# Folding softmax sums to 16 rows per unit by two chains of transfers

## The chip, the cores and the metric

The kernel runs on one core of a Trainium2 chip. Its metric is the device time of one execution in microseconds. The kernel before takes 2106.54 us (median of 3 runs, 2106.08 to 2106.72).

The core has five engines that run beside each other, each through its own list of instructions in order: TensorE (PE, matmuls), VectorE (DVE), ScalarE (ACT), GpSimd (POOL) and SyncE (SP), which here only issues transfers. [...] Memory on the chip has 128 partitions (rows).

## The reference

Two layers on 8 images of 512 channels and 32x32 positions (N = 1024), all in float32. The first is attention with 8 heads, the second a non-local block with a batch norm at its end.

```python
q = _conv1x1(x, Wq, bq).reshape(B, h, d, H * W)
k = _conv1x1(x, Wk, bk).reshape(B, h, d, H * W)
v = _conv1x1(x, Wv, bv).reshape(B, h, d, H * W)
attn = jax.nn.softmax(jnp.einsum('bhdn,bhdm->bhnm', q, k) * scale, axis=-1)
out = jnp.einsum('bhnm,bhdm->bhdn', attn, v).reshape(B, C, H, W)
return x + _conv1x1(out, Wp, bp)
...
f_div_C = jnp.einsum('bcn,bdn->bcd', theta_x, phi_x) / n
y = jnp.einsum('bcd,bdn->bcn', f_div_C, g_x).reshape(b, C_INTER, h, w)
z = _conv1x1(y, W_w, W_b) + x
mean = jnp.mean(z, axis=(0, 2, 3), keepdims=True)
var = jnp.var(z, axis=(0, 2, 3), keepdims=True)
z_hat = (z - mean) * jax.lax.rsqrt(var + EPS)
```

The change is in the softmax alone: in how the sums over the keys, by which the output of attention is divided, are added up.

## The kernel before

The images are taken one after the other. For each, the projections q, v and k are made by products that save multiplications in Strassen's manner (`six`, L377, for the images after the first; each loads its weights by SP in pieces as the ring `wr` comes free, L160 to L175 and L186). Then comes `attention` (L575), then the output projection and the second layer.

Attention goes through 8 units of two heads and 512 queries, and each unit through 8 blocks of 128 keys. For a block TensorE makes the scores with the keys in the rows (L601), ScalarE takes the exponential (L604) into a tile of 128 rows and 2 x 512 columns, and VectorE adds it to the unit's `acc` (L608, L610). TensorE multiplies the exponentials with v (L627). No maximum is taken off; a check of the sums decides at the end whether a second, shifted version has to run.

After a unit's last block, `acc` holds, in each of its 128 rows, sums over 8 keys. The sum over the 128 rows is still to be taken, and `spread` (L642) prepares it: `acc` is cut into four quarters of 32 rows; SP copies the first to 32 rows of the tile `fold` (L638) and POOL adds the other three to it by three transfers (L640), each of which waits until the one before has landed. Unit u goes to the rows from 32 (u mod 4) and to operand u div 4 of the tile, 1024 columns each. So units 0 to 3 fill the 128 rows of one operand, and 4 to 7 those of the next. The last image (`make_f` is set) takes another path for its last unit, and makes its denominators in two halves.

The denominators of an image are then a product with a matrix of zeros and ones (`folds4`, L512), which adds the 32 rows of each unit: `all_denominators` (L670) calls `in_tiles` (L662) with two operands, four matmuls each, one for each quarter of the 1024 columns. A matmul writes 32 rows of `den`. VectorE takes the reciprocals (L678), they go to device memory (L680) and come back spread over the rows (L721), and POOL multiplies the output of attention with them (L707).

This product doesn't stand at the end of attention. It is one of the `fills` of the next image's q (L1107): in `six`, ahead of the third pair of products, two additions are put on POOL (L423, L424) and then the denominators are made. TensorE, VectorE and these POOL additions keep the order of the program (`pe` and `dve`, L62 to L65). Transfers are placed by a scheduler, which leaves each engine a fixed list: on SP, behind the last copy of an image's sums, the first piece of the next k's weights (256 KB) and then two pieces of v's weights (896 KB each); on POOL, the accumulates of all units and then the additions of q.

The tile `fold` has one buffer, `acc` three. `folds4` is made once at the start by VectorE.

Of the kernel before, what the change touches and what calls it, by code (L numbers as in the profile page):

```python
# [8 lines left out]
F32 = mybir.dt.float32  # L9
I32 = mybir.dt.int32  # L10
AF = mybir.ActivationFunctionType
ALU = mybir.AluOpType
# [4 lines left out]
P = 128  # L17
HEADS = 8
# [4 lines left out]
def attention_nonlocal_kernel(tc: tile.TileContext, a: dict, out: bass.AP):  # L23

    sound = unshifted(tc, a, out)
    with tc.If(sound < P):
        shifted(tc, a, out)
# [3 lines left out]
def unshifted(ctx: ExitStack, tc: tile.TileContext, a: dict, out: bass.AP):  # L31
    nc = tc.nc
# [5 lines left out]
    D = C // HEADS  # L38
# [8 lines left out]
    const = ctx.enter_context(tc.tile_pool(name="const", bufs=1))  # L47
# [14 lines left out]
    def pe(ins):  # L62
        tc.keep_in_program_order(ins)

    dve = sp = pe  # L65
# [10 lines left out]
    def block(name):  # L76
        return ring.tile([P, 2, 512], F32, tag="e", name=name)
# [25 lines left out]
    def weight_sums(w, a21, which=(3, 4, 5, 6), pin=lambda ins: None, engine=None):  # L103
        for to, l, r, op in ((3, a21, w[2], ALU.add), (4, w[3], w[0], ALU.subtract),
                             (5, w[0], a21, ALU.subtract), (6, w[1], w[4], ALU.subtract)):
            if to in which:
                pin((engine or nc.vector).tensor_tensor(w[to], l, r, op))
# [83 lines left out]
    def weights(name, sums_done=False, pin=lambda ins: None):  # L191

        w = loaded.pop(0)
        assert w.name == name
        if name not in kept and name != "tp":
            if not sums_done:
                weight_sums(w, corner[name], pin=pin)
            keep("plain" if name == "WpT" else name, w)
        return w
# [42 lines left out]
    def bias_product(t, ps):  # L242
        for oc in range(CC):
            pe(nc.tensor.matmul(ps[:, oc:oc + 1], t[:, oc * P:(oc + 1) * P], ones, start=True, stop=True,
                                skip_group_check=True))
        got = small.tile([P, CC], F32, tag="got", name="got")
        nc.scalar.copy(got, ps)
        nc.vector.tensor_tensor(bp, bp, got, ALU.add)
# [234 lines left out]
    for x_part, w_part in (((0, 1, 0), (w_first[0], 0, 0, 0, 1)), ((1, 2, 0), (w_first[0], 0, 0, 1, 2)),  # L483
# [3 lines left out]
        at = slice(h * 512, (h + 1) * 512)  # L487
        nc.sync.dma_start(xt[:, c0:c1, at], x_v[0, :, c0:c1, at])
        if w_part:
            to, m, k, c0, c1 = w_part  # L490
# [18 lines left out]
    nc.vector.memset(folds8, 0.0)  # L509
    for i in range(4):  # L510
        nc.vector.memset(folds8[i * P // 4:(i + 1) * P // 4, i * 8:(i + 1) * 8], 1.0)
    folds4 = const.tile([P, D], F32, tag="folds4", name="folds4")  # L512
    nc.vector.memset(folds4, 0.0)
    for i in range(4):
        for at in (i * 4, P // 4 + 16 + i * 4):
            nc.vector.memset(folds4[i * P // 4:(i + 1) * P // 4, at:at + 4], 1.0)
    mv = const.tile([P, CC, 2], F32, tag="mv", name="mv")
    ngamma = const.tile([P, CC], F32, tag="ngamma", name="ngamma")
    spill = [dram.tile([P, CC, N], F32, tag=f"spill{b}", name=f"spill{b}") for b in range(B - LATE + 1)]
# [7 lines left out]
    def heads_of(b, what, w, bias, data, pin=lambda ins: None, steps=None, fills=None, **how):  # L527

        t = mats.tile([P, CC, N], F32, tag=what, name=f"{what}_{b}")

        if fills is not None:
            def begin(to, ps, i):
                nc.scalar.activation(to, ps, AF.Identity, bias=bias[:, i:i + 1])

            def third(to, ps, of, i):
                if what == "q":
                    nc.scalar.activation(to, ps, AF.Identity, bias=steps[:, i:i + 1])
                else:
                    dve(nc.vector.scalar_tensor_tensor(to, ps, steps[:, i:i + 1], of, ALU.add, ALU.add))

            six(f"p{what}_{b}", w, data, False, lambda q: t[:, rows(q), cols(q)], begin, third, fills,
                what == "q")
            return t

        def first(q, ps):
            for m in range(2):
                c = rows(q).start + m
                if how.get("early") and q == "21":
                    nc.vector.tensor_scalar(t[:, c, cols(q)], ps[:, m, :], bias[:, c:c + 1], 1.0, ALU.add, ALU.mult)
                else:  # L550
                    nc.scalar.activation(t[:, c, cols(q)], ps[:, m, :], AF.Identity, bias=bias[:, c:c + 1])

        seven(f"p{what}_{b}", w, data, False, first, add_to(t, pin), **how)

        return t
# [19 lines left out]
    def attention(b, q, k, v, near_end, make_f=None):  # L575
# [7 lines left out]
        units = [(p, h) for p in range(NPAIR) for h in range(NH)]  # L583
# [53 lines left out]
        def together(to, parts):  # L637
            nc.sync.dma_start(to, parts[0])  # L638
            for part_of in parts[1:]:
                nc.gpsimd.dma_start(to, part_of, accum_op=ALU.add)  # L640

        def spread(u, pin=lambda ins: None, meanwhile=lambda: None):  # L642

            g, i = divmod(u, 4)
            acc = accs.pop(u).rearrange("p j n -> p (j n)")
            if u == 0:
                folded["t"] = foldp.tile([P, 4, 1024], F32, tag="fold", name=f"fold_{b}")
            t = folded["t"]  # L650
            to = t[i * P // 4:(i + 1) * P // 4]
            parts = [acc[k * P // 4:(k + 1) * P // 4, :] for k in range(4)]
            if make_f and u == len(units) - 1:
                for k in range(4):
                    (nc.scalar if k % 2 else nc.sync).dma_start(to[:, (k + 1) % 4, :], parts[k])
                meanwhile()
                for l, r in ((1, 2), (3, 0), (1, 3)):
                    pin(nc.vector.tensor_tensor(to[:, l], to[:, l], to[:, r], ALU.add))
                return
            together(to[:, g, :], parts)  # L660

        def in_tiles(ps, sums):  # L662

            of = P // 4
            for n, (lhsT, t) in enumerate(sums):
                for i in range(4):
                    pe(nc.tensor.matmul(ps[i * of:(i + 1) * of, :], lhsT, t[:, i * 256:(i + 1) * 256],
                                        start=(n == 0), stop=(n == len(sums) - 1), skip_group_check=True))

        def all_denominators(ps):  # L670

            t = folded.pop("t")
            if b == 0:
                bias_product(t[:, 3, :], ps[:, 1, :CC])
            den = ps[:, 0, :256]
            in_tiles(den, [(folds4[:, g * P // 4:(g + 1) * P // 4], t[:, g, :]) for g in range(2)])
            ri = t[:, 2, :256]
            dve(nc.vector.reciprocal(ri, den))  # L678
            d = dram.tile([P // 4, 256], F32, tag=f"den{b}", name=f"den_d_{b}")
            nc.scalar.dma_start(d, ri.rearrange("(x s) n -> x s n", s=4)[:, 0, :])  # L680
            own.append((slice(b * 64, (b + 1) * 64), d.rearrange("x (y n) -> (x y) n", y=4)))
            return d.rearrange("(j k x) m -> j k (x m)", j=2, k=2)
# [66 lines left out]
        if make_f:  # L749
            return o["o"], lambda ps: denominators(1, ps), lambda d: normalize((first_den, d))  # L750
        return o["o"], all_denominators, normalize

    def project(b, xt, w, between, data):
# [271 lines left out]
    t = [block(f"t{i}_x_0") for i in range(4)]  # L1025
# [17 lines left out]
    k = heads_of(0, "k", wk, bk, data, dve)  # L1043
# [10 lines left out]
    for b in range(B):  # L1054
# [46 lines left out]
        if not last:  # L1101
# [15 lines left out]
            else:  # L1117
                w_p = loaded[1]
                more = [lambda i=i: weight_sums(w_p, corner["WpT"], (i,), dve, nc.gpsimd) for i in (3, 4, 5)]
            k = heads_of(b + 1, "k", weights("WkT"), bk, data, dve, steps=dk, fills={  # L1120
                (0, 13): [*o_sums, *(more if b else ())], (1, 13): () if b else more,
                (2, 0): () if b else [lambda: weight_sums(w_p, corner["WpT"], (6,), dve, nc.gpsimd)]})
# [305 lines left out]
```

## Time and profile before

| what | value |
|---|---|
| median of the runs | 2106.54 us |
| the profiled execution | 2106.07 us |
| its span | 2104.3 us |
| TensorE busy | 2082.4 us, 99% |
| VectorE busy | 1428.2 us, 68% |
| ScalarE busy | 789.9 us, 38% |
| POOL busy | 584.9 us, 28% |
| accumulating transfers of POOL (L640) | 189 of 128 KB, 767 ns of POOL each, 3.0 us to landing (median) |
| copies of SP (L638) | 63 of 128 KB, 2.3 us to landing (median) |
| matmuls of the denominators (L667) | 128 records in 8 images, 379 ns each |

The span reaches from the first to the last instruction of the program; the execution has 1.8 us around it. A float32 matmul[...] has two records. The duration of a matmul is longer than the distance to the next one, since they overlap. In the timeline a line has its start, its length, the engine, the line of the source, the operation and the tiles (out<-in); the brackets give the idle time of the engine before it and what ended that time. For transfers, the length is that of the issue on the engine, and the time from issue to landing is given apart.

### The profile page before, as it was taken

The page shows a single profiled execution, that of the slowest core. Times are in us where ns is not written, and L with a number is a line of the kernel's source. Part 1 is how long each engine was busy: PE and PEld are TensorE (multiplying, and loading weights), DVE is VectorE, ACT ScalarE, POOL GpSimd, SP SyncE. Part 2 cuts the span into 40 slices and gives each one's busy share as a digit, 9 for nine tenths or more (in the row PEclk, how much of TensorE's full clock was granted, in tenths as well). Part 3 has the DMA queues.
Part 4 walks back from the last instruction along what each step waited for, and adds up shares of the span by engine and source line. Part 5 has one row for each costly group of instructions (what it writes and reads, how often), then busy time and mean ns, then how long its engine had stood idle before and what let it go on. Part 6 is the DMA issues. An engine that isn't in the chain of part 4 may idle for free.

```text
span 2104.3 us, 33849 instructions
## 1 busy us (share of the span) xinstructions
PE 2082.4 (99%) x13654; PEld 1172.0 (56%) x13654; DVE 1428.2 (68%) x2144; ACT 789.9 (38%) x1045; POOL 584.9 (28%) x454
## 2 busy tenths in 40 slices
PE   9999999999999999999999999999999999999996
PEld 4535864358733677336773377633876348743472
DVE  6587567775677656876567766677665775656746
ACT  1464204652046410464105631066312653056116
POOL 0012900128101371014611156111560118311010
PEclk9999999999999999999999999999999999999998
DMA  6253534244332432325324253142544235212668
GB/s 230 83 149 76 180 117 143 41 89 150 106 116 39 106 129 105 119 41 137 108 90 121 41 149 115 68 126 41 155 148 154 39 49 173 100 28 40 218 252 321
DMA packets 72884, 246.74 MB, mean 117 GB/s; under 512 B 12817, under 2 KB 21265, under 8 KB 70673
## 3 DMA queue, kind: packets, MB, share of 16 engines
q1 hardware_dynamic: 61792, 218.16, 30.8%
q0 software_dynamic: 9072, 24.78, 9.6%
q8 instruction: 110, 1.80, 0.4%
q10 hardware_dynamic: 1856, 1.56, 0.3%
q14 instruction: 54, 0.43, 0.1%
HBM read 163.20 MB, written 47.71 MB: 100 GB/s over the span
## 4 chain that ended last, share of the span: by engine, by line
PE 98%; ACT 1%; DVE 1%; DMA 0%; issue 0%; DVEq 0%
PE ps L601 21%; PE po L627 21%; PE pp L365 7%; PE ptp L365 7%; PE pv_in L441 6%; PE pq_in L444 6%; PE pk_in L444 6%; PE pg L365 5%; PE pz L365 3%; PE ptp_in_s L313 2%; PE pf L844 2%; PE pp_in_s L316 2%; PE pwf L900 1%; PE pq L411 1%; PE pv L408 1%; PE pv L365 1%
## 5 line engine op out<-in xcount | busy, mean ns | idle before, releaser
L604 ACT ACTIVATE e<-ps 128x1024 f32<-128x1024 f32 x512 | 522.7, 1024 | 422.5 <-PE ps L601 411.8
L610 DVE TENSOR_TENSOR acc<-acc,e 128x1024 f32<-128x1024 f32 x384 | 469.9, 1224 | 102.9 <-ACT e L604 93.2
L601 PE MATMUL ps<-q,k 64*64 64x512 f32 x4096 | 529.3, 589 | 0.0
L627 PE MATMUL po<-e,v 64*64 64x512 f32 x4096 | 528.6, 589 | 0.0
L640 POOL DMA_DIRECT2D fold<-acc x189 | 144.8, 767 | 1181.4 <-DMA fold<-acc 637.7
L627 PEld LDWEIGHTS po<-e,v 64*64 64x64 f32 x4096 | 156.6, 133 | 282.9 <-issue 275.7
L601 PEld LDWEIGHTS ps<-q,k 64*64 64x64 f32 x4096 | 155.5, 133 | 283.5 <-issue 275.6
L888 ACT ACTIVATE g<-pg,gb 128x512 f32<-128x512 f32 x31 | 21.3, 687 | 436.3 <-PE pg L365 436.2
L608 DVE TENSOR_TENSOR acc<-e,e 128x1024 f32<-128x1024 f32 x64 | 78.3, 1224 | 118.4 <-ACT e L604 116.2
L365 PE MATMUL pp<-t_o,w_WpT 128*128 128x512 f32 x208 | 101.0, 592 | 0.0
L365 PE MATMUL ptp<-w_tp,t_x 128*128 128x256 f32 x400 | 96.1, 379 | 0.0
L365 PEld LDWEIGHTS ptp<-w_tp,t_x 128*128 128x128 f32 x400 | 72.3, 190 | 7.8
L452 DVE TENSOR_TENSOR v<-v,pv_in 128x256 f32<-128x256 f32 x112 | 46.2, 421 | 43.8 <-PE pv_in L441 37.3
L452 DVE TENSOR_TENSOR k<-k,pk_in 128x256 f32<-128x256 f32 x112 | 46.7, 421 | 39.5 <-PE pk_in L444 35.4
L365 PE MATMUL ptp<-w_tp,x 128*128 128x256 f32 x272 | 69.6, 380 | 0.0
L365 PE MATMUL pp<-o,w_WpT 128*128 128x512 f32 x144 | 67.7, 592 | 0.0
L450 ACT COPY v<-pv_in 128x256 f32<-128x256 f32 x84 | 31.4, 374 | 95.8 <-DVE T_pv L452 25.5
L450 ACT COPY k<-pk_in 128x256 f32<-128x256 f32 x84 | 31.3, 372 | 91.6 <-PE pk_in L444 90.0
L707 POOL TENSOR_TENSOR o<-o,r 128x1024 f32<-128x1024 f32 x28 | 65.3, 2368 | 0.0
L760 DVE SCALAR_TENSOR_TENSOR x<-pp,bp,x 128x512 f32<-128x512 f32 x52 | 37.6, 746 | 33.0 <-PE pp L365 33.0
L441 PE MATMUL pv_in<-w_WvT,i_t_x 128*128 128x128 f32 x448 | 59.2, 275 | 0.0
L444 PE MATMUL pk_in<-i_t_x,w_WkT 128*128 128x256 f32 x224 | 57.8, 381 | 0.0
(246 smaller groups left out, 3118.5 us busy)
## 6 DMA issues: line engine op xcount, KB each, us to landing
fold<-acc POOLq DMA_DIRECT2D x189, 128.0 KB, 3.0
w_WqT<-kept_WqT SPq DMA_DIRECT2D x21, 896.0 KB, 5.8
w_WvT<-kept_WvT SPq DMA_DIRECT2D x21, 896.0 KB, 5.2
w_WkT<-kept_WkT SPq DMA_DIRECT2D x21, 896.0 KB, 6.1
r<-den_d SPq DMA_DIRECT2D x32, 512.0 KB, 6.8
x<-in_x_dram SPq DMA_DIRECT2D x30, 512.0 KB, 6.0
spill<-x SPq DMA_DIRECT2D x24, 512.0 KB, 4.0
z<-spill SPq DMA_DIRECT2D x24, 512.0 KB, 8.7
```

The source lines that it names most:

```text
L365: pe(nc.tensor.matmul(to_ps, lhsT(k), rhs(k), start=(s, at) not in begun, stop=(k == nk - 1), skip_group_check=True))
L441: pe(nc.tensor.matmul(ps[:, i, :], d[:, i * P:(i + 1) * P], a, start=start and not i, stop=True, skip_group_check=True))
L444: pe(nc.tensor.matmul(ps, a, d, start=start, stop=True, skip_group_check=True))
L450: nc.scalar.copy(piece(q, i, j), ps)
L452: dve(nc.vector.tensor_tensor(piece(q, i, j), piece(q, i, j), ps, ALU.add))
L601: pe(nc.tensor.matmul(ps[c * P // 2:(c + 1) * P // 2, j, :], k[r, p, keys], q[r, p, h * 512:(h + 1) * 512], start=True, stop=True, skip_gr ...
L604: nc.scalar.activation(e, ps, AF.Exp, scale=SCALE)
L608: nc.vector.tensor_tensor(accs[u], es[u, 0], e, ALU.add)
L610: ins = nc.vector.tensor_tensor(accs[u], accs[u], e, ALU.add)
L627: pe(nc.tensor.matmul(ps[j * D:(j + 1) * D, r, :], v[keys, m, (2 * p + j) * D:(2 * p + j + 1) * D], e[keys, j, :], start=(m == 0), stop=(m ...
L640: nc.gpsimd.dma_start(to, part_of, accum_op=ALU.add)
L707: dve((engine or nc.vector).tensor_tensor(at, at, of, ALU.mult))
```

## The change

In images 0 to 6 the sums of a unit are folded to 16 rows instead of 32. `acc` is cut into eight parts of 16 rows. The even parts make one chain, the odd parts another: each starts with a copy of SP and goes on with three accumulates of POOL, 64 KB each. The two chains alternate on POOL, and end in the same 16 rows of two operands of `fold`. All eight units so fill the 128 rows of these two operands. After the last unit POOL adds the second operand to the first, in one instruction of 128x1024, and the product of the denominators has the one operand that is left: four matmuls instead of eight.

`folds4` now adds 16 rows for each unit. Its ones start at multiples of 16 rows; they are written at the start by eight small transfers of POOL from a tile of ones, in place of eight memsets of VectorE. The last image keeps the path it had.

In the order of instructions nothing else moves: TensorE's list is the same without the four matmuls for each image, and those of SP and POOL have the new transfers, and POOL the addition, where the old transfers were.

```diff
-    folds4 = const.tile([P, D], F32, tag="folds4", name="folds4")
+    folds4 = const.tile([P, P // 4], F32, tag="folds4", name="folds4")
     nc.vector.memset(folds4, 0.0)
-    for i in range(4):
-        for at in (i * 4, P // 4 + 16 + i * 4):
-            nc.vector.memset(folds4[i * P // 4:(i + 1) * P // 4, at:at + 4], 1.0)
+    four = const.tile([16, 4], F32, tag="four", name="four")
+    nc.vector.memset(four, 1.0)
+    for i in range(HEADS):
+        nc.gpsimd.dma_start(folds4[i * 16:(i + 1) * 16, i * 4:(i + 1) * 4], four)
...
             t = folded["t"]
+            if not make_f:
+                for k in range(4):
+                    for c in range(2):
+                        to = t[u * 16:(u + 1) * 16, c, :]
+                        of = acc[(2 * k + c) * 16:(2 * k + c + 1) * 16, :]
+                        if k:
+                            nc.gpsimd.dma_start(to, of, accum_op=ALU.add)
+                        else:
+                            nc.sync.dma_start(to, of)
+                if u == len(units) - 1:
+                    dve(nc.gpsimd.tensor_tensor(t[:, 0, :], t[:, 0, :], t[:, 1, :], ALU.add))
+                return
             to = t[i * P // 4:(i + 1) * P // 4]
...
             den = ps[:, 0, :256]
-            in_tiles(den, [(folds4[:, g * P // 4:(g + 1) * P // 4], t[:, g, :]) for g in range(2)])
+            in_tiles(den, [(folds4, t[:, 0, :])])
```

## The prediction

> **What bounds the kernel now.** I read the page's busy times and its chain first, then the instructions of the tiles den and fold, then the timeline around the place where one image's denominators are made, and last the answers on transfers there.
>
> ```profile
> PE 2082.4 (99%) x13654; PEld 1172.0 (56%) x13654; DVE 1428.2 (68%) x2144; ACT 789.9 (38%) x1045; POOL 584.9 (28%) x454
> ...
> PE 98%; ACT 1%; DVE 1%; DMA 0%; issue 0%; DVEq 0%
> ...
> L640 POOL DMA_DIRECT2D fold<-acc x189 | 144.8, 767 | 1181.4 <-DMA fold<-acc 637.7
> ```
>
> TensorE is busy for 99% of the span and is 98% of the chain that ended last. A matmul taken away is time gained, and any moment for which TensorE waits is time lost; nothing else counts. POOL is idle for 72%; its accumulating transfers spend their time waiting for each other.
>
> ```profile
> L667 PE MATMUL den<-fold,folds x128: 379/379/403, 204.0 to 1964.8; 128*32 128x256 f32 x128
> ```
>
> A float32 matmul stands in the trace as two records. 8 images have 16 records each, so 8 matmuls[...].
>
> ```profile
> 447.16 0.51 SPq L638 DMA_DIRECT2D fold<-acc  x1
> ...
> 457.22 6.36 SPq L168 DMA_DIRECT2D w_WvT<-kept_WvT  x2
> ```
> ```profile
> 449.89 0.77 POOL L640 DMA_DIRECT2D fold<-acc  x1 [6.46 <-DMA fold<-acc]
> 452.92 0.77 POOL L640 DMA_DIRECT2D fold<-acc  x1 [2.27 <-DMA fold<-acc]
> 456.24 0.77 POOL L640 DMA_DIRECT2D fold<-acc  x1 [2.55 <-DMA fold<-acc]
> ```
> ```profile
> 463.17 1.07 PE L667 MATMUL den<-fold,folds 128*32 128x256 f32 x16
> 463.30 2.35 POOL L396 TENSOR_TENSOR q<-q 128x1024 f32<-128x1024 f32 x1 [6.29 <-ACT q L450]
> ```
>
> This is the last unit of image 1: SP copies the first quarter of the sums, three accumulates of POOL follow, each when the one before has landed, and TensorE reads the result. I count from SP's issue, F = 447.16. The accumulates are issued at F+2.7, F+5.8 and F+9.1, the last lands 3.3 us later at F+12.4, and the product starts at F+16.0. Its first four matmuls read the units 0 to 3, so unit 7 is needed at about F+16.4: 4.0 us of slack. The other images have the same distances (F+16.0; image 0 F+17.1). At F+10.06 SP issues a weight load of 896 KB. This offset is 10.06 or 10.07 in all seven images.
>
> ```profile
> 965.85 0.77 POOL L640 DMA_DIRECT2D fold<-acc  x1 [7.03 <-DVE i_t_x L273]
> 969.22 0.77 POOL L640 DMA_DIRECT2D fold<-acc  x1 [2.61 <-DMA fold<-acc]
> 972.59 0.77 POOL L640 DMA_DIRECT2D fold<-acc  x1 [2.60 <-DMA fold<-acc]
> ```
> ```profile
> 972.70 6.36 SPq L168 DMA_DIRECT2D w_WvT<-kept_WvT  x2
> ```
> ```profile
> fold<-acc POOLq DMA_DIRECT2D x1, 128.0 KB, 6.2
> ```
>
> Image 3 (F = 962.64) is the warning. Its accumulates run 0.5 to 0.8 us later than elsewhere, the last is issued 0.11 us before the weight load, and it takes 6.2 us to land instead of 3.0 (the page's median). Its packets start at 976.55, when nearly all packets of the load have gone; the load's first packet is at 973.65, 0.95 us after its issue. An undisturbed accumulate has its first packet 1.33 us after its issue, in nearly all of the 189. It would have been at 973.92, 0.27 us too late.
>
> [...] Image 3 shows 2.6 us: the transfer that came second waited for the first. The forecast goes by the trace. [...] accumulates between 32-row blocks of one half (0 to 63, or 64 to 127) land 3.3 us after issue, those from one half to the other 3.0. [...]
>
> **The change part by part.**
>
> 1. Denominators' product, images 0 to 6: 4 matmuls instead of 8. The 16 records of image 1 start in four rounds 0.22 us apart (463.17, 463.41, 463.62, 463.84). Two rounds go: 0.43 us for each image, 7 x 0.43 = 3.0 us, all on TensorE. The change between full and 32-column matmuls leaves 0.1 us on either side of the product; that stays. TensorE's next matmul can take the gain, since the VectorE read that it waits for ends at 463.69.
>
> 2. Eight memsets of VectorE at the start (0.41 us together, at 1.5 us, before an idle time of 7.7 us) become eight transfers of POOL, 16 rows of 16 bytes each. Gain 0. The first 16 us are full of loads, and TensorE waits for weights at 7.84 us, so some 16 small packets on each engine may cost between 0 and 0.8 us; I take 0.2.
>
> 3. SP's copies: two a unit instead of one, 0.51 us of SP each. Between two units SP waits 13 us; behind the last pair the next load is issued 3.9 us later. 0.
>
> 4. POOL's accumulates: 336 instead of 168 in images 0 to 6. Two chains alternate on POOL. The issue itself (0.77 us) is hidden, 168 x 0.77 = 129 us more on an engine with 1500 us idle, and in units 0 to 6 a longer chain meets nobody: an accumulator is written again three units later. What counts is the last unit. Chain 0 keeps its times; chain 1 is 0.77 us behind: F+3.5, then a fast step (rows 48 to 63 onto 112 to 127: other half) F+6.5, then a slow one (80 to 95[...]) F+9.8, landing at F+13.1.
>
> 5. The added POOL add, 128x1024 float32: 2.36 us by the equal adds (L396). It waits for both chains: F+13.1 to F+15.5, and TensorE sees it at about F+15.55. The single operand makes the first matmul need all units, so F+16.0 counts, not F+16.4. The slack shrinks from 4.0 to 0.45 us. POOL's q adds stand behind it, with 2.6 us idle after their second; TensorE needs nothing of POOL's until 50 us later. 0 for these.
>
> 6. Hence the question: does the last accumulate still get ahead of the weight load? Before, its packets start at F+9.1+1.33 = F+10.4, and the load's at F+11.0: 0.6 us to spare. After: F+9.8+1.33 = F+11.1. It comes 0.1 us too late, in every image, as the offsets repeat. An earlier race has the same shape: chain 1's first accumulate has packets at F+4.8, and the 256 KB load issued at F+3.86 arrives at F+4.8; losing that one adds about 1.2 us and loses the second for certain.
>
> 7. If it is lost, image 3 gives the price. Packets start at 976.55 = F+13.9 and end at F+15.6 with two rows for each engine; with one row, about F+15.1. 0.65 us later (as everywhere between last packet and next issue) the add starts, F+15.75, ends at F+18.1, and TensorE starts at F+18.2 instead of F+16.0: 2.2 us late, less the 0.43 gained, 1.75 us for each image. Bounds: [...]2.65 if the packets take as long as image 3's.
>
> Sum: images 1 to 6, 6 x 1.75 = 10.5; image 0, product at F+17.1, 1.1 - 0.43 = 0.65; start 0.2. That is +11.4 us. The profiled execution takes 2106.07 us (span 2104.3, 1.8 around it), so 2117.5; the median of the runs shown is 0.47 higher: 2106.54 + 11.4 = 2117.9 us.
>
> **The rivals.**
>
> A. The add is hidden. 16 rows may take POOL a little less than 0.77 us and their packets less time, four issues follow each other on chain 1, and 0.1 us for each is enough: packets at F+10.7, before the load. Then every step of 5 holds: -3.0 + 0.2, 2103.7 us. For it: the margin is a tenth of a microsecond and 32-row durations are all I have. Against it: the packets must be ahead on all 16 engines, and they are spread over 0.2 us. It decides at packets before about F+10.9.
>
> B. The forecast, 2117.9 us.
>
> C. Some images win and others lose, by the jitter that image 3 shows (0.45 us at its first accumulate): three lost of seven, 3 x 1.75 - 4 x 0.43 + 0.2 = +3.7, 2110.3 us.
>
> D. Faster by more than A: both gaps of 0.1 us around the product go as well, 7 x 0.2 = 1.4 more: 2102.3 us. Nothing speaks for it[...].
>
> E. The change does not do what it says: the build would chain every accumulate to the one before it, whichever chain it is of. The instruction order shows each waiting for its own chain's transfer, so I give it nothing apart; it would end as B, later.
>
> **How the numbers follow.** B 0.50, A 0.37, C 0.10, D 0.03. A difference of 0.2% is 4.2 us, about what a measurement of this kernel can tell from no change. B is slower by 0.54%; A (-0.13%) is within; C is split, 0.07 slower and 0.03 same; D is faster. So slower 0.57, same 0.40, faster 0.03. B's own range is 2113 to 2121.7: below, half of the images lose only a part; above, 2.65 us late, 6 x 2.2 + 1.1 + 0.8 for the start = 15.1. The range must hold A as well: A with nothing lost at the start is 2103.5, so 2103.2 to 2121.5.
>
> **What would show it.** Right: 8 records of den in images 0 to 6; TensorE idle before den in these, released by the POOL add; the add starts near F+15.8; the last accumulate lands some 6 us after issue, with its packets after those of w_WvT. Wrong: the add ends before F+16.0 and den starts there. Then the step that failed is 6. If the add is late without the load in the way, it is the durations of 4.

## The result, and the profile of the changed kernel

| | before | changed |
|---|---|---|
| median of the runs | 2106.63 us (2106.08 to 2107.09, 4 runs) | 2128.53 us (2126.70 to 2130.61, 4 runs) |
| ratio | | 1.0105, 95% interval 1.0093 to 1.0117 |
| the profiled execution, its span | 2106.07, 2104.3 us | 2128.25, 2126.5 us |

The change makes the kernel 1.05% slower: 21.9 us, where the forecast had 11.4. The time lies above the range that was given (2103.2 to 2121.5). The direction and the mechanism of the wait are those of the forecast; a part of the price was not in it.

First the page of the changed kernel: the busy times, the head of the chain that ended last, and the accumulates among the costliest groups.

```profile
PE 2087.6 (98%) x13598; PEld 1175.5 (55%) x13598; DVE 1427.6 (67%) x2137; ACT 790.9 (37%) x1045; POOL 734.1 (35%) x637
...
PE 91%; DMA 5%; ACT 1%; DVE 1%; POOL 1%; issue 1%; POOLq 0%; DVEq 0%
...
L658 POOL DMA_DIRECT2D fold<-acc x336 | 257.3, 818 | 953.7 <-DMA fold<-acc 456.1
...
fold<-acc POOLq DMA_DIRECT2D x336, 64.0 KB, 3.0
```

TensorE had 98% of the chain and now has 91%: the accumulating transfers, which had next to nothing, have 5%. (The chain follows a wait back through all that led to it, so these 5%, some 100 us, are not the loss.) The last line is the one to remember: an accumulate of 64 KB lands in 3.0 us, just as one of 128 KB did.

The instructions of the tile den, with the idle time of their engines and who ended it:

```profile
L680 PE MATMUL den<-fold,folds x72: 379/391/404, 206.3 to 1986.4; 128*32 128x256 f32 x72
...
  POOL fold L662: 35.5, 14
```

There are 72 records: 8 in each of the images 0 to 6 and 16 in image 7, as the change wants. But TensorE stands still before the product in every image. (The 35.5 us in 14 waits count the matmuls and the weight loads of TensorE apart; the matmuls' 7 waits, 16.5 us, are what counts here.) Before, no product waited for POOL.

The chain that ended last, through the end of image 2's attention. Here F = 712.71, the time at which SP issues the copies of the last unit. Columns: start, length, what.

```profile
712.71 2.27 DMA fold<-acc
...
716.19 3.86 DMA fold<-acc
720.05 0.28 issue
720.33 3.08 DMA fold<-acc
723.41 0.28 issue
723.69 4.92 DMA fold<-acc
...
728.77 2.34 POOL fold L662
731.12 0.04 issue
731.16 0.64 PE den L680 x8
```

And SP's queue in the same stretch:

```profile
712.71 1.14 SPq L660 DMA_DIRECT2D fold<-acc  x2
716.57 0.33 SPq L168 DMA_DIRECT2D w_WkT<-kept_WkT_first  x1
722.77 6.36 SPq L168 DMA_DIRECT2D w_WvT<-kept_WvT  x2
```

This is the second of the two chains. Its first accumulate (716.19 = F+3.48) meets the 256 KB load (716.57) and takes 3.86 us to land; its last (723.69 = F+10.98) is issued 0.92 us after the first 896 KB load and takes 4.92 us. Only the middle one goes undisturbed, in 3.08 us. The addition starts at F+16.06, ends at F+18.4, and TensorE starts the product at F+18.45. Before, it started at F+16.0.

The timeline of TensorE there:

```profile
727.76 1.03 PE L444 MATMUL pq_in<-i_t_x,w_WqT 128*128 128x256 f32 x4
731.16 0.64 PE L680 MATMUL den<-fold,folds 128*32 128x256 f32 x8 [2.38 <-POOL fold L662]
```

The gap from the start of one matmul to the start of the next is 2.75 us here, against 0.31 before. In the images 0 to 6 these gaps are 1.91, 3.31, 2.75, 2.63, 2.84, 2.80 and 2.75 us. Less the usual 0.31 (0.50 in image 0), that is 16.6 us of standstill.

There is a second loss, which the busy times hide, since a slow matmul is a busy one. Stretches of the changed kernel around the products of the images 1 and 2; columns: stretch, its length, busy time and number of instructions of PE, PEld, DVE, ACT and POOL, then the granted clock of TensorE, the share of the DMA engines and their GB/s.

```profile
466.80:470.64 3.84, 0.92 (x10) 0.49 (x11) 0.64 (x2) 0.00 (x0) 3.31 (x2) 1.00 0.66 234
470.65:474.05 3.40, 3.40 (x10) 2.69 (x9) 1.53 (x1) 1.58 (x4) 3.32 (x2) 0.50 0.03 11
474.06:478.00 3.94, 3.94 (x20) 3.47 (x19) 2.53 (x6) 1.06 (x4) 0.33 (x1) 1.00 0.33 85
728.80:732.00 3.20, 0.84 (x9) 0.43 (x10) 0.55 (x2) 0.00 (x0) 3.20 (x2) 1.00 0.71 228
732.00:735.40 3.40, 3.40 (x17) 2.94 (x17) 1.97 (x2) 2.44 (x6) 3.32 (x2) 1.00 0.16 64
```

After image 1's standstill the granted clock is 0.50 for 3.41 us: 10 matmuls where image 2 has 17. This happens in the images 0, 1, 5 and 6, and costs 1.7 us each time (TensorE's lag behind the kernel before grows by 1.69, 1.68, 1.69 and 1.69 us within these stretches). After the images 2, 3 and 4 it doesn't happen.

The whole difference of the two spans, 22.2 us, so has these parts, each read as the lag of equal matmuls against the kernel before: standstill 16.6; half clock 4 x 1.7 = 6.8; four matmuls less in each of seven images, -3.0; the start 0.9; 0.35 at one place in the last image; the end of the program 0.6. That is 22.2.

### The profile page after: what moved, and what is told of

It reads as the page before. It is cut to its first block, busy times and chain, and to the rows that moved or that the text cites. A ratio compares the mean times of both kernels' runs of the same rounds, so it can differ in the third digit from the quotient of the medians.

```text
span 2126.5 us, 34152 instructions
## 1 busy us (share of the span) xinstructions
PE 2087.6 (98%) x13598; PEld 1175.5 (55%) x13598; DVE 1427.6 (67%) x2137; ACT 790.9 (37%) x1045; POOL 734.1 (35%) x637
## 4 chain that ended last, share of the span: by engine, by line
PE 91%; DMA 5%; ACT 1%; DVE 1%; POOL 1%; issue 1%; POOLq 0%; DVEq 0%
PE ps L602 21%; PE po L628 20%; PE pp L365 7%; PE ptp L365 7%; PE pv_in L441 6%; PE pk_in L444 6%; DMA fold<-acc 5%; PE pg L365 5%; PE pz L365 3%; PE pq_in L444 2%; PE ptp_in_s L313 2%; PE pf L857 2%; PE pp_in_s L316 2%; PE pwf L913 1%; PE pq L365 1%; PE pv L408 1%
## 5 line engine op out<-in xcount | busy, mean ns | idle before, releaser
L658 POOL DMA_DIRECT2D fold<-acc x336 | 257.3, 818 | 953.7 <-DMA fold<-acc 456.1
L444 PE MATMUL pq_in<-i_t_x,w_WqT 128*128 128x256 f32 x224 | 63.0, 408 | 0.0
```

What stands on the lines that cost most here:

```text
L444: pe(nc.tensor.matmul(ps, a, d, start=start, stop=True, skip_group_check=True))
L658: nc.gpsimd.dma_start(to, of, accum_op=ALU.add)
```

## The experiments

The theory after this reading: accumulates of the second chain queue up behind SP's weight loads; the addition of 2.3 us then stands in the open; and a standstill at the wrong moment costs the clock on top. The rivals: the addition or the longer chain alone is too slow, with loads or without; or the transfers' number weighs on the whole kernel.

**The loads held back.** A copy of 16 bytes from the addition's result to device memory is put on SP, ahead of the two 896 KB loads in one kernel, and ahead of the 256 KB load as well in the other. SP issues in order, so the loads wait until the addition is done (image 2 of the second kernel: the addition ends at 721.61, the copy is issued at 721.64, the loads at 721.99 and 722.41). Nothing else changes.

```diff
+    def hold():
+        t = kept_back.pop("t", None)
+        if t is not None:
+            n = len(kept_back)
+            kept_back[n] = dram.tile([1, 4], F32, tag=f"hold{n}", name=f"hold{n}")
+            sp(nc.sync.dma_start(kept_back[n], t[:1, 0, :4]))
...
             load_w("first")
+            hold()
...
                     dve(nc.gpsimd.tensor_tensor(t[:, 0, :], t[:, 0, :], t[:, 1, :], ALU.add))
+                    kept_back["t"] = t
```

In the second kernel `hold()` stands one place earlier, ahead of the call that issues the 256 KB load.

> The changed kernel, with both loads of 896 KB that follow an image's sums on SP held back until the POOL add has ended (a copy of 16 bytes from its result stands ahead of them on SP); the load of 256 KB stays where it was. Theory (the last accumulate of chain 1 waits for the load of 896 KB): it lands 3.3 us after its issue again, at about F+14.5, the add ends at F+16.7 to F+17.0 instead of F+18.3 to F+19.0, TensorE is 0.7 to 1.0 us late instead of 2.2 to 3.0, and less the 0.43 gained the sum is 2 to 4 us: about 2109.5. Rival (the chains are too long in themselves, the loads don't matter): as the changed kernel, 2128.

Measured: 2111.55 us (2110.62 to 2113.93, 11 runs), the kernel before beside it 2106.83; ratio 1.0023 (1.0014 to 1.0032).

> As the one before, with the load of 256 KB held back too. Theory: both chains run at the pace of undisturbed accumulates, the last lands at about F+13.4, the add ends at F+15.8, before the product's place at F+16.0; TensorE waits for nothing and the gain of 7 x 0.43 us is left: 2103.6. Rival: 2128.

Measured: 2105.49 us (2104.79 to 2106.09, 12 runs); ratio 0.9994 (0.9985 to 1.0003).

So the loads in the way are what makes the change slow. Counted against the kernel before, the changed kernel is 21.9 us above, the first of these 4.7 above and the second 1.3 below: the 896 KB loads cost 17.2 us, the clock's share in them, and the 256 KB load 6.1. (The split belongs to this order of holding; the 256 KB load held back alone was not run.) POOL in image 2 of the second kernel (F = 705.82), to be laid beside the chain above:

```profile
711.80 1.64 POOL L667 DMA_DIRECT2D fold<-acc  x2 [1.62 <-DMA fold<-acc]
715.03 0.76 POOL L667 DMA_DIRECT2D fold<-acc  x1 [1.59 <-DMA fold<-acc]
715.99 0.76 POOL L667 DMA_DIRECT2D fold<-acc  x1 [0.20 <-issue]
719.26 2.35 POOL L671 TENSOR_TENSOR fold<-fold 128x1024 f32<-128x1024 f32 x1 [2.51 <-DMA fold<-acc]
```

The steps of the second chain in image 2, from F, in us:

| | forecast | changed | 896 KB held | all held |
|---|---|---|---|---|
| first accumulate issued | 3.5 | 3.48 | 3.41 | 3.48 |
| second | 6.5 | 7.62 | 7.88 | 6.86 |
| third | 9.8 | 10.98 | 11.25 | 10.17 |
| the addition starts | 15.75 | 16.06 | 14.51 | 13.44 |
| the product starts | 18.2 | 18.45 | 16.92 | 16.19 |

Without loads the addition ends at F+15.7 to F+15.8, in image 1 at F+16.1, and the product is 0.2 us later than before at most (in the images 3 to 6 it starts at F+16.0). With the 256 KB load alone in the way, the addition comes 0.8 to 1.2 us later, and TensorE waits for 0.6 to 1.2 us in the images 1 to 6.

The gain left is 1.3 us and not 3.0. The trace of the kernel with all loads held has the 0.43 us in each image. Against it stand 0.6 us at the end of the program and four small delays of TensorE (0.33, 0.14, 0.17 and 0.35 us): -3.0 + 1.0 + 0.6 = -1.4. A gain of 0.06% is below what can be told from no change; that this version beats both is not shown.

**The same hold in the kernel before.** It shows what the hold itself costs. There it waits for the last accumulate, since there is no addition.

```diff
             together(to[:, g, :], parts)
+            if not make_f and u == len(units) - 1:
+                kept_back["t"] = t
...
         free[:] = tags
+        hold()
```

> The kernel before, with the same copy ahead of the same three loads (it waits for the last accumulate, there is no add). It tells whether later loads cost or gain anything by themselves. Both theories: 2106.6, within 1 us.

Measured: 2106.66 us (2105.86 to 2107.46, 12 runs) beside 2106.83; ratio 1.0000 (0.9991 to 1.0008). The loads start at F+12.6 to F+13.1 and F+13.0 to F+13.6 here instead of F+3.86 and F+10.06, and no cost of that can be seen. In the two kernels above they start some 4 us later still, which this control does not reach; if that has a price, the race costs so much more than the two show.

**No addition, two operands.** The two chains stay; the product reads both operands, with eight matmuls, as before. The addition is left out.

```diff
-                if u == len(units) - 1:
-                    dve(nc.gpsimd.tensor_tensor(t[:, 0, :], t[:, 0, :], t[:, 1, :], ALU.add))
...
-            in_tiles(den, [(folds4, t[:, 0, :])])
+            in_tiles(den, [(folds4, t[:, g, :]) for g in range(2)])
```

> The changed kernel without the POOL add: the product takes both operands, eight matmuls. Theory: the last accumulate still loses against the loads and lands at F+15.9 to F+16.6, but the operand of chain 1 is needed only at F+16.4, so TensorE is 0 to 0.2 us late and nothing is gained: 2106.6 to 2108. Rival (the 64 KB transfers cost TensorE in another place than at this product): 2115 or more.

Measured: 2108.16 us (2107.28 to 2108.52, 12 runs); ratio 1.0006 (0.9997 to 1.0015). In its trace the chains lose the same races (last accumulate at F+10.9 to F+11.4), and still no product waits: in the images 1 to 6 all start at F+16.0. The lost race alone is within the slack; it needs the 2.35 us of the addition to become a loss. Its trace is 1.2 us longer than that of the kernel before: the 0.35 in the last image and the 0.6 at the end that the changed kernel has too, and 0.2 at the start.

**More work for POOL in the kernel before.** Two, then three additions of 128x1024 on POOL between the last accumulate and the product; the last one works on the second operand in place, and the others make the zeros for it, so that the sums are the same. One chain of 32 rows, as before.

```diff
             together(to[:, g, :], parts)
+            if not make_f and u == len(units) - 1:
+                one, nil = t[:, 1, :], t[:, 2, :]
+                dve(nc.gpsimd.tensor_tensor(nil, one, one, ALU.subtract))
+                dve(nc.gpsimd.tensor_tensor(one, one, nil, ALU.add))
```

> The kernel before, with two POOL additions of 128x1024 between the last accumulate and the product (the sums stay the same). No transfer is changed. They take 4.7 us from F+12.4, so the product's second half, needed at F+16.4, has to wait until F+17.1: 0.7 us for each of images 1 to 6, none for image 0: +4.2, 2110.8. The granted clock stays at full speed by both theories[...].

Measured: 2116.47 us (2115.33 to 2117.30, 4 runs) beside 2106.60; ratio 1.0047 (1.0030 to 1.0063). That is 9.9 us, more than expected. The trace says why. In the images 1 to 5 the second half of the product comes 0.33 to 1.13 us later after the first than it did, as it should; image 6 is another matter. POOL and SP there (F = 1727.74):

```profile
1730.98 0.77 POOL L640 DMA_DIRECT2D fold<-acc  x1 [7.08 <-DVE i_t_x L273]
1734.37 0.77 POOL L640 DMA_DIRECT2D fold<-acc  x1 [2.63 <-DMA fold<-acc]
1737.71 0.77 POOL L640 DMA_DIRECT2D fold<-acc  x1 [2.58 <-DMA fold<-acc]
1744.24 1.89 POOL L663 TENSOR_TENSOR fold<-fold 128x1024 f32<-128x1024 f32 x1 [5.76 <-DMA fold<-acc]
```
```profile
1737.81 0.33 SPq L168 DMA_DIRECT2D w_WvT<-kept_WvT  x1
```

The chain runs 0.5 to 0.8 us late from its first accumulate on, as image 3 of the kernel before did in the prediction; why it starts late is open. The last accumulate is issued 0.10 us before the load, loses to it all the same, and lands after 6.4 us. The product's second half stands still for 4.21 us, and half clock follows (1.6 us more; the mean granted clock of this execution is 0.995, that of the kernel before 0.996). An undisturbed image in the same execution has its first addition at F+12.4, this one at F+16.5: the lost race costs the chain 4.1 us. In this trace it came about in one image of seven, with nothing changed in the chain. The other three runs are as long (2115.33 to 2117.30 us), but what made them so no trace shows. The 4.1 us are the price of the race in the kernel before too, where the slack pays for it.

> The same with three POOL additions: TensorE is 3.0 us late in images 1 to 6 and 1.9 us in image 0, 20 us in all, without any change of the transfers. Theory (a stall of 2 to 3 us in some images also halves the granted clock for 3.4 us, which costs 1.7 us each time): three to six such times, 5 to 10 us more: 2131 to 2137. Rival (the stall alone counts): 2126.6.

Measured: 2131.47 us (2130.24 to 2133.97, 4 runs); ratio 1.0119 (1.0102 to 1.0136). With the clock's loss the time is where it was expected, and 5 us above the rival without it. In its trace the first and the last matmul record of a product are 2.20 to 4.36 us apart instead of 0.69, 17.1 us more in all; half clock follows in five of the seven images, 8 us (mean granted clock 0.992); the start has 0.9. The sum, 26.0, is the difference of the spans (2130.2 - 2104.3 = 25.9).

The images 3 and 4 of this kernel are nearly twins. Both stand still between the halves, at the same place of the program:

```profile
994.43 0.64 PE L672 MATMUL den<-fold,folds 128*32 128x256 f32 x8 [2.15 <-POOL fold L665]
...
1254.84 0.64 PE L672 MATMUL den<-fold,folds 128*32 128x256 f32 x8 [2.16 <-POOL fold L665]
```

The four stretches of half clock in the changed kernel's trace last 3.413 us each and start a whole number of such lengths apart (with a step of 3.4133 us, 1511.71 and 470.64 are 305.0 steps apart, 1760.88 and 207.82 are 455.0). So do two of this kernel, after the images 1 and 4 (470.74 and 1255.80, 230.0 steps). Cut along this grid, the images 3 and 4 look like this (columns as above):

```profile
989.56:992.97 3.41, 2.71 (x18) 1.69 (x17) 2.06 (x6) 0.37 (x1) 3.25 (x3) 1.00 0.24 50
992.97:996.38 3.41, 1.95 (x14) 1.33 (x15) 1.18 (x1) 0.64 (x2) 3.41 (x2) 1.00 0.64 250
996.39:999.80 3.41, 3.41 (x17) 3.00 (x17) 2.02 (x5) 1.79 (x5) 2.66 (x2) 1.00 0.03 10
1252.38:1255.79 3.41, 1.25 (x18) 0.52 (x11) 0.37 (x2) 0.00 (x0) 3.35 (x2) 1.00 0.77 252
1255.80:1259.21 3.41, 3.41 (x10) 2.70 (x9) 1.57 (x1) 1.65 (x4) 3.33 (x2) 0.50 0.04 15
1259.22:1262.62 3.40, 3.40 (x18) 2.98 (x17) 2.15 (x6) 0.88 (x3) 0.30 (x1) 1.00 0.22 82
```

In image 4 all 2.16 us lie in one step, 63% of it, and the next step runs at half clock. In image 3 the grid's line falls into the standstill: TensorE is idle for 0.70 us of one step and 1.46 of the next (21% and 43%), and the clock stays. The price of the same standstill is 1.6 us in one case and nothing in the other.

**The array kept busy.** The changed kernel with four matmuls on constant data ahead of each product, which nobody reads.

```diff
+    idle = const.tile([P, 256], F32, tag="idle", name="idle")
+    nc.vector.memset(idle, 1.0)
...
+            for i in range(4):
+                pe(nc.tensor.matmul(ps[:, 0, 256:], idle[:, :P], idle, start=True, stop=True))
             in_tiles(den, [(folds4, t[:, 0, :])])
```

> The changed kernel, with four matmuls of 128x256 on constant data put on TensorE ahead of each of the seven products of denominators. They write a part of PSUM that nobody reads, and depend on nothing that is late, so they run while TensorE would stand still (1.66 to 2.93 us in the trace of the changed kernel; four of them take 1.7 us). The transfers, the addition and the time at which the sums are ready stay as they are. Theory: the four stretches of half clock, 3.41 us each, which follow the standstill in that trace, cost 1.7 us each and are brought about by the idle array. With the array busy none of them comes: 2128.5 - 6.8 = 2121.7 us, clock granted in full from the start to the last product, and the products of denominators no later relative to the sums. Rival: the half clock has another cause, or its price is already in the waits: 2128.5 us as before.

Measured: 2122.22 us (2121.67 to 2122.36, 4 runs) beside 2106.45; ratio 1.0076 (1.0059 to 1.0092). TensorE does more work and the kernel is 6 us faster. The mean granted clock is 0.996, as in the kernel before, where the changed kernel has 0.993. TensorE at image 1's product, and then two stretches there (columns as above):

```profile
465.49 1.89 PE L692 MATMUL den<-idle 128*128 128x256 f32 x8
468.16 0.64 PE L682 MATMUL den<-fold,folds 128*32 128x256 f32 x8 [0.78 <-POOL fold L664]
```
```profile
465.50:469.50 4.00, 3.22 (x21) 2.17 (x20) 1.05 (x2) 0.16 (x2) 3.73 (x2) 1.00 0.68 231
469.50:473.50 4.00, 4.00 (x20) 3.46 (x19) 2.54 (x5) 2.40 (x6) 3.28 (x2) 1.00 0.03 10
```

The product still waits for the addition, but only 0.78 us are idle, and what comes next goes at full clock (1.00). So in this kernel the half clock goes when the array is kept busy, and the share of it in the changed kernel's loss is measured: 15.8 us are left of 21.9. (The 6.1 us between them are near the 6.8 of the clock less what the four matmuls cost by themselves: in image 0 they end after the addition, and the product starts 0.5 us later than it did, at F+19.0.) The spread shrinks as well, from 3.9 us to 0.7: a stretch of half clock more or less in the other runs of the changed kernel, 1.7 us each, would account for it (an estimate from their mean granted clocks, 0.992 to 0.993).

**More transfers for POOL.** The kernel before with each accumulate of units 0 to 6 cut into four of 256 columns, to test whether the number of POOL's transfers is what lengthens the end of the program.

```diff
-            together(to[:, g, :], parts)
+            if make_f or u == len(units) - 1:
+                together(to[:, g, :], parts)
+                return
+            nc.sync.dma_start(to[:, g, :], parts[0])
+            for part_of in parts[1:]:
+                for n in range(4):
+                    at = slice(n * 256, (n + 1) * 256)
+                    nc.gpsimd.dma_start(to[:, g, at], part_of[:, at], accum_op=ALU.add)
```

> The kernel before, with each accumulating transfer of POOL cut into four of 256 columns each for the units 0 to 6 of images 0 to 6 (3 x 49 x 3 = 441 transfers more, the same bytes and sums); the last unit of each image, whose chain races with the weight loads, stays as it was. Theory: in the changed kernel POOL's last instruction, which closes its queue, takes 10.10 us instead of 5.61 for 176 more transfers, 25.5 ns each, and ends 0.6 us after everything else. By that, 441 more take 11.2 us more, POOL ends 10.5 us later than SP's last store allows now less the 3.7 us for which it was hidden: about 7.1 us, 2113.8 us, all of it behind TensorE's last matmul. Rival: the closing instruction waits for something else, and the number of POOL's transfers costs nothing while POOL has idle time: 2106.7 us.

Measured: 2107.65 us (2107.06 to 2107.97, 12 runs) beside 2106.45; ratio 1.0006 (0.9997 to 1.0014). The expectation was wrong. The instruction that closes POOL's queue takes 5.614 us in the kernel before, with 189 transfers, 10.101 us in the changed kernel, with 365, and 2.102 us in this one, with 630. It does not grow with the number, and what sets it stays open. The traces show only that it ends last in those with 365 transfers, and that their ends come 0.5 to 0.7 us later than before, counted from TensorE's last matmul: in the changed kernel it runs from 1.7 to 11.8 us after the end of TensorE's last matmul, while SP is through at 11.1. Nor do 441 transfers more cost anything else that can be told from nothing: the trace has 1.1 us more at the start, and 0.8 in small delays.

## Why the prediction was right and wrong

- **Step 1, the product's four matmuls: right.** 8 records in each of the images 0 to 6, two rounds of 0.22 us less: TensorE's lag falls by 0.43 us at each product, also in the kernel with all loads held, where nothing covers it.
- **Step 2, the start: no cost of the transfers that can be seen.** The changed kernel's trace is 0.9 us behind at 28.7 us, where 0.2 was taken (0 to 0.8). But the start differs between executions with either form: 1.1, 0.3, 0.9 and 1.1 us behind in the traces with the memsets (the hold in the kernel before, two and three additions, more transfers), 0.9, 0.4, 1.3, 0.2 and 0.9 in those with the eight transfers (changed, 896 KB held, all held, two operands, array kept busy). The transfers make no difference that can be seen, and the trace of the kernel before, which the sum was made against, is one with an early start.
- **Step 3, SP's second copy: right.** 0.
- **Step 4, the chain's times: too early.** The first accumulate of the second chain is at F+3.5 as forecast. But the race with the 256 KB load, which was priced at 1.2 us and not put into the sum, is lost in every image: the second accumulate goes at F+7.6 to F+8.1 instead of 6.5, the third at F+11.0 to F+11.4 instead of 9.8. And without any load it is F+10.1 to F+10.2: 64 KB in 16 rows take as long to land as 128 KB in 32 (a median of 3.0 us in both profiles). By itself this would already have been enough: 10.15 + 1.33 is past the load's first packet at F+11.0. Two readings were off as well, without weight in the sum: the 3.3 and 3.0 us of the old accumulates lie between one issue and the next, and to landing they take 3.1 and 2.75; and the last one of image 1 landed 4.2 us after its issue, at F+13.3, not at F+12.4.
- **Step 5, the addition: right.** 2.34 us instead of 2.36. On an undisturbed chain it ends at F+15.8 (forecast 15.5), inside the slack but in image 1 (F+16.1). The additions of q behind it delayed nothing that TensorE waited for.
- **Step 6, the race with the 896 KB load: right,** and by more than was thought. The kernel with these loads held shows it: 17.2 us of the 21.9 are gone. Rivals A and C, in which all or some images win, are out: all seven lose. Rival E too: the second chain's first accumulate is issued 0.6 to 0.7 us behind the first chain's, before that one has landed.
- **Step 7, the price: too low, and one term was missing.** The product starts at F+18.3 to F+19.0, with a median of F+18.5, instead of 18.2; image 0 is 1.4 us late instead of 1.1. That the chain comes to the load 1.2 to 1.6 us later than forecast is not the reason: the last accumulate's packets begin at F+13.5 to F+13.6 in all seven images, whenever it was issued (forecast 13.9), and end at F+15.0 to F+15.7 (15.1). What was sized too small is the time from there to the start of the addition: 0.9 us in five of the seven images (0.5 and 1.2 in the others) where 0.65 was taken. In sum TensorE stands still for 16.6 us where 14.3 were forecast (6 x 2.2 + 1.1). The largest miss is what isn't in the sum at all: half clock after four of the seven standstills, 6.8 us, of the 10.8 by which the two traces exceed the forecast. The other misses count too: without half clock (the array kept busy) the kernel takes 2122.2 us, still 0.7 above the range. The 0.6 us at the end of the program and 0.35 in the last image were not there either.

The forecast's 11.4, with 2.3 for the standstill, 6.8 for the clock, 0.7 for the start and 1.0 for the end and the last image, is the 22.2 that the two traces show.

The step that failed is 7, in what it left out: the clock. It took a standstill to cost its own length, and put nothing for what TensorE does after it; the runs show 1.7 us more after four of seven. The length of a standstill alone does not tell which: in the changed kernel TensorE is idle for 1.66, 2.93, 2.42 and 2.37 us ahead of the products of the images 0, 1, 5 and 6, which half clock follows, and for 2.38, 2.25 and 2.47 us in the images 2, 3 and 4, which none follows. The images 3 and 4 with three additions show that the place of a standstill on the grid goes with the price; what else decides it is open.

## What to carry to other kernels

Price a transfer chain together with what the other queues issue in the same microseconds: here the slack of 4 us was enough for the longer chain with the loads in the way, and for the longer chain and the addition without them, but not for all three; when loads are not urgent, a tiny transfer ahead of them that waits for the chain's result takes them out of the race (in the kernel before, at no cost that could be seen: ratio 1.0000). Halving the bytes of a small transfer by halving its rows need not make it faster (3.0 us for 64 KB here, as for 128 KB): look at the time to landing, not at the KB. And the standstills of TensorE, 1.66 to 2.93 us in the changed kernel, cost up to 1.7 us each on top, by where they fell, so allow up to that much for every one of that kind, or fill the wait with idle matmuls (6 us less here).

## What the runs showed that was not expected

- The clock's loss after a standstill, and that two equal standstills of 2.15 us have different prices (0 and 1.6 us) at different places on a grid of 3.413 us.
- Giving TensorE 28 useless matmuls makes the changed kernel 6 us faster (2128.5 to 2122.2 us).
- An accumulate that is issued before a load can still lose to it: at 0.10 us ahead it landed after 6.4 us instead of 3.1. An undisturbed accumulate's first packet comes 1.33 us after its issue and the load's 0.95 (image 3 of the kernel before; 0.98 to 1.06 for the 256 KB loads of the changed kernel), so a lead of 0.4 us looks like enough; but the second chain's first accumulates, up to 0.47 us ahead of the 256 KB load, all lost. Their packets begin over 0.5 us (1.33 to 1.84 us after the issue, undisturbed), the first 16 of the 32 packets of an old one over 0.2.
- The closing instruction of POOL's queue takes 5.614 us with 189 transfers (before), 10.101 with 365 (changed) and 2.102 with 630, and it ended the program where it took 10.101.
